# One graph layer on one core: three comparison tiles with a buffer each, the third listed a turn earlier

## The chip, the core and the metric

The kernel runs on one core of one Trainium2 chip. Its time is the device time of one execution in microseconds (us), given as the median of several runs. Below, TensorE is PE, VectorE is DVE, ScalarE is ACT, GpSimd is POOL and the DMA-issuing sync engine is SP, as in the profile.

## What is computed

The reference is one layer of a graph network with a residual and a normalisation. There are 12500 nodes with 128 features, and 400000 edges sorted by their target:

```python
Xs = X[src]
m_data = Xs @ W_data.T + b_data
m_ctrl = Xs @ W_control.T + b_control
msg = jnp.where((edge_types == 0)[:, None], m_data, m_ctrl)
agg = jax.ops.segment_sum(msg, dst, num_segments=X.shape[0])
out = relu(agg + (X @ W_self.T + b_self))
x = layernorm(X + out)
```

Both products are linear, so the kernel sums the raw rows of X first, separately for the two edge types, and multiplies the sums by the weights once for each node.

## The kernel before, in words

**Two ways to fetch a row.** The edges are cut into chunks of 128. Of each 25 chunks, 5 (or, at some places, more) are fetched from memory row by row by indirect DMAs that POOL issues (`msg`, line 825). The other 20 form a *set*, and their rows are picked out of a copy of X that stays in SBUF, by matmuls with 0/1 matrices. There are 107 sets, and the loop `for w in range(pairs)` treats one after the other. Rows are held as three bfloat16 parts, so 128 features are 384 columns.

**Ordering a set.** A set's 2560 edges are first put in order by the 128-row block of X that their source lies in. DVE compares block numbers (`O`, line 533 by way of `block_matrix`), adds up (`prod`, lines 614, 615 and 604), PE counts what stands ahead (line 624), DVE reduces that (`ahead`, line 632) and works out a rank (lines 636 to 645), builds `rm` (line 533) and `rv` (line 676), and PE scatters with them (line 688). ACT copies the result out (`cell`, line 696), SP sends it through memory and spreads it over all partitions (`pick`, line 701), and DVE turns it in place into a 0/1 matrix (`pick`, line 743). This preparation is done two to three sets ahead of use; the last step, line 743, is done during the set before. Edges for which there was no room are found by `key` (line 649) and `top` (line 653), and are moved over by a small chain DVE `over_n` (660), PE (552), DVE `om_all` (558), PE (564), ACT, and one indirect DMA (`both`, line 901) for two sets.

**Using a set.** `picked(w, ...)` makes five turns (`unit(t)`, t from 0 to 4) and an end. `bounds = [0, 5, 10, 15, 19, 24]` are the groups of columns, out of 25, that each turn handles. In turn t:

- PE picks the rows of group t (line 926, four matmuls of 32 output rows for each column) into PSUM tiles `got`, and ACT copies those to SBUF as `emsg` (line 940).
- DVE makes the selection matrices for a number of columns with one comparison each (`choose`, line 917, which calls `select`, line 533): out of `code_col` and the set's `code` it writes a tile `esel` of 128 x (columns x 176). The *first* comparison, listed in turn 0, covers columns 0 to 9 (128x1760). The *second*, in turn 1, covers 10 to 18 (128x1584). The *third*, in turn 3, covers 19 to 24 (128x1056).
- PE adds the previous group's rows into the set's PSUM tile `sums` (line 757, three matmuls a column), with `emsg` and `esel`. Turn 1 reads columns 0 to 4, turn 2 columns 5 to 9, turn 3 columns 10 to 14, turn 4 columns 15 to 18. Columns 19 to 24 are read by the end of the set, `end()`, which the next set's turn 0 calls (`ending()`) after its own first comparison. There DVE also adds `sums` into `acc` (line 814).

**The buffers of the comparisons.** `esel` tiles come from a pool with two buffers for each name. The third comparison takes the buffer of the first of its set, the next set's first that of the second, the next set's second that of the third. A comparison can start when PE has done the last matmul that reads the buffer's previous tile.

**Other work on DVE between them.** The selection matrices of the fetched chunks (`psel`, line 533, 128x1200), their sums and counts (`cnt` and `acc`, line 814), preparation of a group's indices (lines 494 to 515), and finished nodes (lines 1054 to 1071).

**What sets the order.** A program lists the instructions: for each set, several streams (turns, preparation, `pick` of the next set, indices) carry a place between 0 and 1, and `merged` lists them by it. The turns stand at 0.1, 0.3, 0.5, 0.7 and 0.9, the rank chain at 0.31 to 0.35, `O` and lines 614, 615 and 604 at 0.55, line 743 at 0.6, lines 649 and 653 at 0.75. Then a planner of the framework fixes each engine's order when the kernel is compiled: it takes instructions in the listed order, but where the next one is not ready in its plan (an input is missing, a buffer is not free) it takes the first later one that is. `tc.issue_after(...)` forbids some of that: lines 614, 615, 604 and 743 may not come ahead of the latest `rv`. On the chip each engine then keeps the fixed order. The gathers of POOL are gated one by one by matmuls of PE (`paced`).

Of the kernel before, what the change touches and what calls it, by code (L numbers as in the profile page):

```python
# [9 lines left out]
BF = mybir.dt.bfloat16  # L10
# [9 lines left out]
P = 128  # L20
# [17 lines left out]
EW = 88  # L38
# [113 lines left out]
def evenly(units, a=0.0, b=1.0):  # L152
    return [(a + (b - a) * (k + 0.5) / len(units), u) for k, u in enumerate(units)]
# [53 lines left out]
def short_path(ctx, tc, const, ident, eps, wT, brow, bad, x, src, dst, etype, ws, bs, out):  # L207
# [127 lines left out]
    def table(n, base, name):  # L335

        t = keep.tile([P, n], BF, name=name)
        nc.vector.tensor_copy(t, iota([n], [[1, n]], base, 0, f"{name}_i"))
        return t
# [8 lines left out]
    code_col = table(2 * EW, 1, "code_col")  # L348
# [177 lines left out]
    slots, placed = {}, []  # L526
    pairs = len(each_e)

    def select(sel, col, code2):

        rows, n, width = sel.shape
        shape = [rows, n, width // 2, 2]
        nc.vector.tensor_tensor(  # L533
            sel.rearrange("p n (w t) -> p n w t", t=2),
            col[:rows].rearrange("p (o w t) -> p o w t", o=1, t=2).to_broadcast(shape),
            code2.rearrange("p n (o t) -> p n o t", o=1).to_broadcast(shape),
            op=OP.is_equal,
        )
        return sel
# [209 lines left out]
    def sums():  # L749
        return ps2.tile([P, 512], FP, name="sums")  # L750

    def cells_of(ps, width, k):
        return ps[:, k * 2 * width:(k + 1) * 2 * width]

    def add_rows(out, msg, sel, start, stop):
        for j in range(3):
            last = nc.tensor.matmul(  # L757
                out, msg[:, j * D:(j + 1) * D], sel, start=(start and j == 0), stop=stop, skip_group_check=True
            )
        return last  # L760
# [39 lines left out]
    def acc_rows(g, a, b):  # L800
        begin_acc(g)
        return acc[g][:, a:b, :]

    def place_of(g, i):

        parts_in[g] = parts_in.get(g, 0) + 1
        with tc.issue_after(added[-2].ins) if len(added) > 1 else ExitStack():
            return nc.vector.value_load(raw["place"][0:1, g, i:i + 1], min_val=0, max_val=R - WMAX)

    def accumulate(at, rows, ps, wide, width):  # L810

        n = rows.shape[1]
        win = rows[:, :, bass.ds(at, width)]
        added.append(nc.vector.tensor_add(win, win, ps[:, :n * wide].rearrange("p (a w) -> p a w", w=wide)[:, :, :width]))  # L814
# [15 lines left out]
    def paced(now, gate):  # L830

        if spare:
            gather = spare.pop()()
        elif to_fetch and due[len(due) - len(to_fetch)] <= now:
            gather = fetch()
        else:
            return
        tc.add_manual_dep(
            gather.ins, gate.ins.name,
            mybir.DependencyInfo(mybir.DependencyClass.Sync, mybir.DependencyReason.DATA), reason="paced",  # L840
        )
# [8 lines left out]
    def count(ps, sel):  # L850

        for r in range(FAR):
            n = len(range(r, CHUNKS, FAR))
            at = 2 * AW + DPC * r
            for t in range(2):
                nc.tensor.matmul(
                    ps[CAP * t:CAP * (t + 1), at:at + n * PW], one_col[:, :CAP], sel[:, r::FAR, t * PW:(t + 1) * PW],
                    start=False, stop=(r == FAR - 1), skip_group_check=True,
                )
# [35 lines left out]
    def spare_rows(w):  # L895
        n = P if w + 1 < pairs else OVF
        both = two.tile([P, 3 * D], BF, name="both", bufs=1)
        slots[w + 1 if n == P else w]["last"] = both
        if n == P:
            slots[w]["both"] = both  # L900
        return nc.gpsimd.indirect_dma_start(  # L901
            out=both[:n, :], out_offset=None, in_=rows3[:, :],
            in_offset=bass.IndirectOffsetOnAxis(ap=slots[w]["idx"][:n], axis=0),
        )

    def picked(w, tiled, ending, before):

        g, i = each_e[w]  # L910
        s = {"sel": {}, "msg": {}}
        bounds = [0, 5, 10, 15, 19, NQ - 1]
        turns = len(bounds) - 1

        def choose(q0, n):

            sel = select(sp.tile([P, 10, 2 * EW], BF, name="esel")[:, :n], code_col, slots[w]["code"][:, q0:q0 + n])
            for k in range(n):
                s["sel"][q0 + k] = sel[:, k]

        lead = 0 if w % 2 else 2
        half_rows = slice(CAP * lead, CAP * lead + OVF)

        def pick(ps, q, a0=0, a1=4):
            for a in range(a0, a1):
                last = nc.tensor.matmul(  # L926
                    ps[CAP * a:CAP * (a + 1), :], slots[w]["pick"][:, a * NQ + q, :],
                    x3[:, 4 * q + a - a0].rearrange("p j d -> p (j d)"), start=True, stop=True, skip_group_check=True,
                )
            return last  # L930

        def rows(q, n, room, half=False):
            ps = psg.tile([P, room, 512], FP, name=f"got{room}")
            msg = two.tile([P, room, 3 * D], BF, name=f"emsg{room}")
            for k in range(n):
                last = pick(ps[:, k, :3 * D], q + k)
                s["msg"][q + k] = msg[:, k, :]
            if half:
                last = pick(ps[:, n, :3 * D], NQ - 1, lead, lead + 2)
            s["out"] = nc.scalar.copy(msg[:, :n], ps[:, :n, :3 * D])  # L940
            if half:
                nc.scalar.copy(s["msg"][NQ - 1][half_rows, :], ps[half_rows, n, :3 * D])
            return last

        def add(q0, q1):
            done = [
                add_rows(cells_of(s["ps"], EW, 0), s["msg"].pop(q), s["sel"][q], q == 0, q == NQ - 1)
                for q in range(q0, q1)
            ]
            return done[len(done) // 2 - 1], done[-1]  # L950

        def unit(t):

            if t == 3:
                assert not spare
                if "both" in slots[w]:
                    slots[w]["last"] = two.tile([P, 3 * D], BF, name="last", bufs=1)
                s["msg"][NQ - 1] = slots[w]["last"]
            paced(w + (t + 0.5) / turns, rows(bounds[t], 2, 2))
            if t == 1 and w > 0 and w % 2 == 0:  # L960
                spare.append(lambda: spare_rows(w))
            gate = rows(bounds[t] + 2, bounds[t + 1] - bounds[t] - 2, 3, t == 3)
            if t == 0:
                choose(0, 10)
                gates = ending() or [gate]
            if t == 1:
                choose(10, 9)
            if t == 3:
                choose(19, NQ - 19)
            while counts:  # L970
                c = counts.pop(0)
                count(c["ps"], c["sel"])
            if t == 1:
                s["ps"] = sums()
            if t == 1 and before:
                before()
            if t > 0:
                gates = add(bounds[t - 1], bounds[t])
            paced(w + (t + 1) / turns, gates[0])
            if t == 2:  # L980
                paced(w + (t + 1) / turns, gates[-1])
            for u in tiled.get(t, []):
                u()
            if t == 0 and w + 1 < pairs and "own_turn" in slots[w + 1] and w > 0:
                slots[w + 1]["own_turn"]()
            if t == turns - 1 and "both" in slots[w]:
                with tc.issue_after(s["out"].ins):
                    nc.scalar.copy(slots[w]["last"][:OVF, :], slots[w]["both"][:OVF, :])

        def end():  # L990

            early, *more = tiled.get(turns, [lambda: None])
            early()
            gates = add(bounds[turns - 1], NQ)
            for u in more:
                u()
            accumulate(place_of(g, 2 * i + 1), acc_rows(g, 0, 2), s["ps"], EW, EW)
            return gates

        return evenly([lambda t=t: unit(t) for t in range(turns)]), end  # L1000


# [139 lines left out]
    sp = ctx.enter_context(tc.tile_pool(name="sel", bufs=2))  # L1142
# [13 lines left out]
    n = 0  # L1156
# [11 lines left out]
    def ending():  # L1168
        pass
# [191 lines left out]
```

## Time and profile before

| what | value |
|---|---|
| median of 3 runs | 1719.61 us (1719.46 to 1721.19) |
| the profiled execution | 1721.01 us |
| its span, first to last instruction | 1719.3 us |
| granted TensorE clock, mean | 0.994 |
| busy: PE, PE weight loads, DVE, ACT, POOL | 1568.1, 1241.5, 1529.0, 1243.3, 1286.8 us |

The time outside the span is 1721.01 - 1719.3 = 1.7 us. A line such as `L533 DVE TENSOR_TENSOR esel<-code_col,code 128x1760 bf16<-... x321 | 292.9, 913 | 11.8 <-PE sums L757 8.8` reads: line 533, engine DVE, the tile that is written and those that are read, the shape, how many; busy us in all and mean ns of one; then how long the engine sat idle just before these instructions and what ended most of that.

### The profile page before, as it was taken

To read this page: it belongs to the slowest core of one execution; us is meant where nothing else is said; L and a number is where in the kernel's file an instruction comes from. 1 tells how busy PE (TensorE), PEld (TensorE's weight loads), DVE (VectorE), ACT (ScalarE), POOL (GpSimd) and SP (SyncE) were. 2 spreads that over 40 slices of the span, in tenths; PEclk is the share of its full clock that TensorE was granted. 3 is DMA by queue.
4 is the path that set the end of the run, shared out by engine and by line. 5 is a ranking of instruction groups with operands and counts; after the bars stand their busy time and mean duration, and the time that the engine had idled before them with its cause. 6 is when DMAs were issued, how large, how long until landed. Compare 5 with 4: busy or idle time off the path is not lost.

```text
span 1719.3 us, 68641 instructions
## 1 busy us (share of the span) xinstructions
PE 1568.1 (91%) x28525; PEld 1241.5 (72%) x28525; DVE 1529.0 (89%) x3630; ACT 1243.3 (72%) x2198; POOL 1286.8 (75%) x1061
## 2 busy tenths in 40 slices
PE   0599999999999999999899999999999999999997
PEld 0377777777777777777677777777777777777776
DVE  6899899998998989999799899999999899999983
ACT  5777677776777667777576777676777676777675
POOL 0288878888788888888788777777788787777872
PEclk9999999999999999999999999999999999999999
DMA  7844454545444454444445554545544445544442
GB/s 195 280 149 133 126 160 124 147 147 152 134 139 142 139 148 135 140 150 129 144 122 150 160 155 136 152 130 152 150 144 138 135 128 159 155 140 129 138 128 59
DMA packets 148973, 248.30 MB, mean 144 GB/s; under 512 B 35937, under 2 KB 115260, under 8 KB 148652
## 3 DMA queue, kind: packets, MB, share of 16 engines
q1 hardware_dynamic: 85994, 134.45, 23.6%
q0 software_dynamic: 50032, 102.98, 22.2%
q10 hardware_dynamic: 12626, 6.40, 1.4%
q8 instruction: 225, 3.69, 0.9%
q14 instruction: 96, 0.79, 0.1%
HBM read 226.24 MB, written 17.50 MB: 142 GB/s over the span
## 4 chain that ended last, share of the span: by engine, by line
DVE 40%; PE 38%; issue 8%; ACT 5%; DMA 4%; DVEq 1%; POOL 0%; SPq 0%; ACTq 0%; POOLq 0%
PE sums L757 16%; PE got L926 12%; DVE esel L533 5%; DVE prod L641 5%; DVE prod L636 4%; DVE rv L676 3%; DVE pick L743 3%; DVE found L643 3%; PE side L1045 3%; ACT emsg L940 2%; DVE prod L614 2%; PE side L624 2%; DMA both<-rows,idx 2%; DVE psel L533 2%; PE side L688 2%
## 5 line engine op out<-in xcount | busy, mean ns | idle before, releaser
L825 POOL DMA_INDIRECT msg<-rows,idx_g x985 | 1215.5, 1234 | 309.7 <-issue 143.8
L940 ACT CAST emsg<-got 128x768 bf16<-128x768 f32 (+1 forms) x1070 | 949.0, 931 | 296.9 <-PE got L926 277.8
L757 PE MATMUL sums<-esel,emsg 128*128 128x176 bf16 x7704 | 686.6, 240 | 3.4 <-DVE acc L814 2.9
L757 PEld LDWEIGHTS <-emsg 128*128 128x128 bf16 x7704 | 569.5, 98 | 106.1 <-issue 98.8
L926 PE MATMUL got<-x,pick 128*32 128x384 bf16 x10486 | 569.1, 330 | 17.9 <-ACT emsg L940 8.8
L926 PEld LDWEIGHTS <-pick 128*32 128x32 bf16 x10486 | 240.4, 96 | 143.8 <-issue 19.9
L533 DVE TENSOR_TENSOR esel<-code_col,code 128x1760 bf16<-128x1760 bf16 x321 | 292.9, 913 | 11.8 <-PE sums L757 8.8
L757 PE MATMUL sums<-psel,msg 128*128 128x48 bf16 x2955 | 167.2, 184 | 11.8 <-DVE acc L814 9.0
L757 PEld LDWEIGHTS <-msg 128*128 128x128 bf16 x2955 | 138.6, 97 | 21.2 <-issue 16.4
L641 DVE TENSOR_TENSOR prod<-prod 128x1200 bf16<-128x1200 bf16 x214 | 134.0, 626 | 7.2 <-issue 1.1
L533 DVE TENSOR_TENSOR O<-cell_col,blk 128x2000 bf16<-128x2000 bf16 x107 | 128.0, 1197 | 7.1 <-ACT blk L439 4.3
L636 DVE TENSOR_TENSOR prod<-O,ahead 128x2000 bf16<-128x2000 bf16 x107 | 128.3, 1200 | 4.5 <-DVE ahead L632 1.9
L743 DVE TENSOR_SCALAR pick<-pick,lane_f 128x3200 bf16<-128x3200 bf16 x107 | 112.9, 1055 | 0.1
L901 POOL DMA_INDIRECT both<-rows,idx x54 | 66.2, 1226 | 54.4 <-ACT emsg L940 41.8
L688 PE MATMUL side<-rv,O 128*128 128x64 bf16 x2140 | 83.4, 195 | 25.0 <-DVE rv L676 22.1
L533 DVE TENSOR_TENSOR psel<-near_col,near 128x1200 bf16<-128x1200 bf16 x125 | 96.7, 773 | 9.7 <-issue 8.7
L814 DVE TENSOR_TENSOR acc<-acc,sums 128x176 f32 (+2 forms) x232 | 66.8, 288 | 42.1 <-PE sums L757 41.3
L688 PEld LDWEIGHTS <-O 128*128 128x128 bf16 x2140 | 79.0, 100 | 27.2 <-DVE rv L676 22.3
L676 DVE TENSOR_TENSOR rv<-rm,vals 128x1280 bf16<-128x1280 bf16 x107 | 87.9, 822 | 3.3 <-DVE key L649 1.4
L643 DVE TENSOR_REDUCE found<-prod 128x20 f32<-128x600 bf16 x107 | 82.9, 775 | 3.2 <-DVE prod L641 0.4
L614 DVE TENSOR_TENSOR prod<-O 128x1000 bf16<-128x1000 bf16 x107 | 72.0, 673 | 0.0
L624 PEld LDWEIGHTS <-ltri 128*128 128x128 bf16 x1284 | 40.4, 96 | 40.0 <-issue 38.5
(196 smaller groups left out, 1544.6 us busy)
## 6 DMA issues: line engine op xcount, KB each, us to landing
pick<-there SPq DMA_DIRECT2D x106, 800.0 KB
msg<-rows,idx_g POOLq DMA_INDIRECT x985
acc<-acc_start SPq DMA_DIRECT2D x23, 640.0 KB
rows<-x SPq DMA_DIRECT2D x6, 1344.0 KB
xs<-in_x_dram SPq DMA_DIRECT2D x99, 62.5 KB
out_dram<-h SPq DMA_DIRECT2D x99, 62.5 KB
xt<-in_x_dram ACTq DMA_DIRECT2D x6, 896.0 KB
cnt<-cnt_start SPq DMA_DIRECT2D x22, 160.0 KB
```

What stands on the lines that cost most here:

```text
L533: nc.vector.tensor_tensor(sel.rearrange("p n (w t) -> p n w t", t=2), col[:rows].rearrange("p (o w t) -> p o w t", o=1, t=2).to_broadcast( ...
L614: nc.vector.tensor_add(h[:, :2 * CQ], s["O"][:, :2 * CQ], s["O"][:, 2 * CQ:])
L636: nc.vector.tensor_tensor(prod[:, :, :NCELL], s["O"], ahead.rearrange("p (o j) -> p o j", o=1).to_broadcast([P, EC, NCELL]), op=OP.mult,)
L641: nc.vector.tensor_add(prod[:, :, :h], prod[:, :, :h], prod[:, :, h:2 * h])
L643: nc.vector.tensor_reduce(found, prod[:, :, :h], AX.X, OP.add)
L676: placed[:] = [nc.vector.tensor_tensor(rv.rearrange("p c v (r t) -> p c v r t", t=2), rm.rearrange("p c (o r t) -> p c o r t", o=1, t=2).t ...
L688: nc.tensor.matmul(s["rk"][:m, :2 * CAP], s["held"][:, c * NCELL:c * NCELL + m], s["rv"][:, c].rearrange("p v r -> p (v r)"), start=(c == ...
L743: nc.vector.tensor_scalar(t, t, lane_f, None, op0=OP.is_equal)
L757: last = nc.tensor.matmul(out, msg[:, j * D:(j + 1) * D], sel, start=(start and j == 0), stop=stop, skip_group_check=True)
L825: return nc.gpsimd.indirect_dma_start(out=msg, out_offset=None, in_=rows3[:, :], in_offset=bass.IndirectOffsetOnAxis(ap=codes["p", g][0][: ...
L926: last = nc.tensor.matmul(ps[CAP * a:CAP * (a + 1), :], slots[w]["pick"][:, a * NQ + q, :], x3[:, 4 * q + a - a0].rearrange("p j d -> p (j ...
L940: s["out"] = nc.scalar.copy(msg[:, :n], ps[:, :n, :3 * D])
```

## The change

The `esel` tiles get three buffers in place of two, so each of a set's three comparisons always has the same buffer, and shares it only with the same comparison of other sets. The third comparison is listed in turn 2 in place of turn 3. Nothing else is edited.

```diff
         def choose(q0, n):
-            sel = select(sp.tile([P, 10, 2 * EW], BF, name="esel")[:, :n], code_col, slots[w]["code"][:, q0:q0 + n])
+            sel = select(sp.tile([P, 10, 2 * EW], BF, name="esel", bufs=3)[:, :n], code_col, slots[w]["code"][:, q0:q0 + n])
...
             if t == 1:
                 choose(10, 9)
-            if t == 3:
+            if t == 2:
                 choose(19, NQ - 19)
```

## The prediction

> **What bounds the kernel now.** I read the page's busy times first, then the busy time of each engine in the steady stretch from 100 to 1700 us, then what PE and DVE waited for there, and last one set in the timeline. Below, A, B and C are the first, second and third comparison of a set.
>
> ```profile
> PE 1568.1 (91%) x28525; PEld 1241.5 (72%) x28525; DVE 1529.0 (89%) x3630; ACT 1243.3 (72%) x2198; POOL 1286.8 (75%) x1061
> ```
> ```profile
> 100.00:1700.00 1600.00, 1516.43 (x27774) 1203.50 (x27772) 1443.90 (x3373) 1168.69 (x2092) 1262.46 (x1024) 0.99 0.47 141
> ```
>
> In the steady stretch PE is idle for 1600 - 1516 = 84 us, 5%; DVE for 156 us. Time can only be won where PE idles, and it is lost wherever DVE makes PE wait longer. So the next view is what PE waited for in that stretch (us in all, times, longest):
>
> ```profile
> PE side L709 <- ACT cell L696: 19.2, 12, 6.3
> PE sums L757 <- DVE acc L814: 12.0, 19, 1.1
> PE side L504 <- DVE code_r L496: 11.6, 17, 1.1
> PE got L926 <- DVE pick L743: 8.1, 17, 1.0
> PE got L926 <- ACT emsg L940: 7.5, 22, 0.6
> PE side L564 <- DVE om_all L558: 6.4, 21, 0.7
> PE side L552 <- DVE over_n L660: 3.9, 6, 0.9
> ```
>
> No row has `esel`: PE never waits for a comparison. It waits, by half a us at a time, for what DVE does after them: `pick`, `om_all`, `over_n`, `code_r`, `acc`. DVE's own waits in the stretch:
>
> ```profile
> DVE acc L814 <- PE sums L757: 40.4, 35, 7.7
> DVE ahead L632 <- PE side L624: 30.3, 53, 1.6
> DVE esel L533 <- PE sums L757: 8.8, 20, 2.1
> ```
>
> The wait that the change removes is the last, 8.8 us in 20 times. Here is what DVE did in a set without other work, from its start to the start of the next (start, duration, and in brackets the idle time before it and what ended that, where it was 0.15 us or more):
>
> ```profile
> 1235.64 1.06 DVE L533 TENSOR_TENSOR esel<-code_col,code 128x1760 bf16<-128x1760 bf16 x1
> 1236.63 1.22 DVE L533 TENSOR_TENSOR O<-cell_col,blk 128x2000 bf16<-128x2000 bf16 x1
> 1237.77 0.39 DVE L558 TENSOR_SCALAR om_all<-slot_col,side 128x70 bf16<-128x70 bf16 x2
> 1238.08 0.33 DVE L814 TENSOR_TENSOR acc<-acc,sums 128x176 f32 x1
> 1238.33 0.97 DVE L533 TENSOR_TENSOR esel<-code_col,code 128x1584 bf16<-128x1584 bf16 x1
> 1240.26 0.37 DVE L632 TENSOR_REDUCE ahead<-side 128x100 bf16<-128x200 f32 x1 [0.96 <-PE side L624]
> ...
> 1244.26 0.49 DVE L533 TENSOR_TENSOR rm<-rank_col,rank 128x640 bf16<-128x640 bf16 x1
> 1244.66 0.70 DVE L533 TENSOR_TENSOR esel<-code_col,code 128x1056 bf16<-128x1056 bf16 x1
> 1245.28 0.82 DVE L676 TENSOR_TENSOR rv<-rm,vals 128x1280 bf16<-128x1280 bf16 x1
> ...
> 1247.22 1.05 DVE L743 TENSOR_SCALAR pick<-pick,lane_f 128x3200 bf16<-128x3200 bf16 x1
> 1248.19 0.17 DVE L649 SCALAR_TENSOR_TENSOR key<-rank,pk 128x20 f32<-128x20 bf16 x1
> ...
> 1248.49 1.06 DVE L533 TENSOR_TENSOR esel<-code_col,code 128x1760 bf16<-128x1760 bf16 x1
> ```
>
> and from PE's rows of that stretch (the last matmul group of turn 2, that of turn 4, the first use of the next set's `pick`):
>
> ```profile
> 1238.22 0.51 PE L564 MATMUL side<-bits_b,om_all 128*128 128x3 bf16 x14 [0.37 <-DVE om_all L558]
> ...
> 1242.38 1.31 PE L757 MATMUL sums<-esel,emsg 128*128 128x176 bf16 x15
> ...
> 1247.03 1.08 PE L757 MATMUL sums<-esel,emsg 128*128 128x176 bf16 x12
> ...
> 1248.80 1.00 PE L926 MATMUL got<-x,pick 128*32 128x384 bf16 x20
> ```
>
> Two things are to be seen. The listed order isn't DVE's: `O`, listed at 0.55, runs right behind A, and C, listed behind `pick`, stands ahead of `rv`. The planner pulls forward whatever is ready when the next in the list isn't. And DVE is a close second bound: `pick` ends at 1247.22 + 1.05 = 1248.27, PE needs it at 1248.80, a cover of 0.53 us; 17 sets have none (the row of L926 and L743 above).
>
> **The change part by part.** Durations are the means of these groups:
>
> ```profile
> L533 DVE TENSOR_TENSOR O<-cell_col,blk 128x2000 bf16<-128x2000 bf16 x107 | 128.0, 1197 | 7.1 <-ACT blk L439 4.3 <-issue 1.5 <-PE side L552 0.8
> L533 DVE TENSOR_TENSOR esel<-code_col,code 128x1760 bf16<-128x1760 bf16 x107 | 113.7, 1062 | 5.4 <-PE sums L757 2.8 <-PE side L688 1.0 <-PE side L709 0.5
> L533 DVE TENSOR_TENSOR esel<-code_col,code 128x1584 bf16<-128x1584 bf16 x107 | 104.4, 975 | 0.1
> L533 DVE TENSOR_TENSOR esel<-code_col,code 128x1056 bf16<-128x1056 bf16 x107 | 75.0, 701 | 6.2 <-PE sums L757 6.0
> ```
>
> No instruction is added or removed and none changes its shape; no DMA is issued by the moved step, and it passes only DVE's queue. What changes is when each comparison may start. C waited for turn 2's matmuls, which read A (1242.38 + 1.31 = 1243.69), and started at 1244.66, at the first opening behind that. Now it waits for the previous set's end, as `acc` does: it may run from 1238.4 on. The *next* set's A waited for turn 4's matmuls, which read B (1247.03 + 1.08 = 1248.11); now it waits for turn 2's, so it may run from 1243.69 on, inside this set's rank chain. B waited for the end's matmuls; now for turn 4's, so it may run ahead of `acc`.
>
> 1. *The waits of `esel`*, 8.8 us, go. C's part, 6.0 us, lies ahead of `rv` and `pick`. PE gains only where `pick` has no cover, 17 of 106 sets, and little cover in some more: I count a quarter, -1.5 us (bounds 0 and -8.8).
>
> The Trainium skill, Perfetto Trace Analysis, § Optimization Strategy, says that the same gap repeating on the engine that should be saturated can mean that there isn't enough SBUF for the next tile, that is, too few buffers. By that rule the extra buffer would be worth those 8.8 us, 1719.6 - 8.8 = 1710.8. The rows of PE's waits speak against it, as the gap is DVE's.
>
> 2. *C leaves the chain, B and O change places.* C's 0.70 us disappear ahead of `rv`. B, listed ahead of `O`, now takes the place ahead of `acc`. Behind `acc` then stand C and O, 0.70 + 1.20 = 1.90 us, where B's 0.975 stood: +0.92. Where DVE idles ahead of `ahead` that is hidden: 30.3 us in 53 waits, 0.57 in each, 0.29 as a mean over 106 sets. So `pick` moves by -0.70 + 0.92 - 0.29 = -0.07 us, say -0.06. (Where O stays ahead of `acc` it is -0.70; where no idle hides O, +0.22.)
>
> 3. *A is pulled into the chain of the set before.* No row shows that, since its buffer wasn't free. Nearest is C, which waited for just the same matmuls: in this stretch it stands inside the chain. Where A takes that place, `pick` is 1.06 us later. From below: never, as line 649 (0.17 us) is listed ahead of A and can fill the opening between `rm` and `rv`. From above: in every set. I take 0.4 of the sets: nearest to the row of C, less what line 649 takes. `pick` moves by +0.42 us in the mean.
>
> 4. *What that costs.* Together `pick` is 0.36 us later. In 17 sets without cover that is 17 x 0.36 = 6.1 us. For the other 89 I estimate a cover spread evenly from 0 to 1 us around the 0.53 read above: 89 x 0.36 x 0.36 / 2 = 5.8 us. `code_r` stands behind `rv` and moves too, in sets that partly pay already: 17 x 0.36 / 2 = 3.1 us.
>
> 5. *What it gives back.* An A that ran early no longer stands ahead of `om_all` and `over_n`: 0.4 of (6.4 + 3.9) = -4.1 us. In the others B for O makes `om_all` 0.22 us earlier: 0.6 x 21 x 0.22 = -2.8 us. What of `acc` gets late behind B is inside the 40.4 us that DVE waits there: 0, with a cost of B's 0.975 in sets where DVE arrives late.
>
> Sum: -1.5 + 6.1 + 5.8 + 3.1 - 4.1 - 2.8 = **+6.6 us**. The profiled execution is 1721.0 us (span 1719.3 + 1.7 outside), 1.4 above the median, so it would become 1727.6, and the median 1719.6 + 6.6 = **1726 us**, 0.4% slower. If A is pulled forward in 0.6 of the sets (`pick` +0.58), the same sum is 9.9 + 15.0 + 4.9 - 6.2 - 1.9 - 1.5 = +20, 1740 us. In none it is -1.0 - 4.6 - 1.5 = -7, 1712.5 us. It changes sign at about a quarter of the sets.
>
> **The rivals.**
>
> - *Faster: C fills real idle time.* C goes into the idle before `ahead`, O stays ahead of `acc`, and A stays behind `pick`. Then `pick` and `code_r` are 0.70 us earlier in the half of the sets that have that idle; half of PE's 8.1 and 11.6 us goes, with the 4.6 and 1.5 from above: -4 - 5 - 4.6 - 1.5 = -15, so 1705 to 1712, middle **1708**. For it: 30.3 us of idle at just that place. Against: gains end where PE's waits end, and the planner fills openings that the chip doesn't have as readily as real ones (C at 1244.66 stands in one behind `rm`, which ends at 1244.26 + 0.49 = 1244.75). It decides when A overtakes `pick` in under a quarter of the sets.
> - *No change.* C has long been ahead of `pick`, so its new place in the list does nothing, and A, B and O only trade places within cover: within 3.4 us of **1719.6**.
> - *Much slower: B and O both ahead of `om_all`.* PE stands 0.37 us at L564 for it in the quoted set. With another 0.975 us ahead, in half of the 53 sets that have it (one chain for two sets): +26, **1745**. For it: `om_all` is just in time. Against: one comparison already fills the opening that O filled.
> - *DVE is the bound.* Then all idle that C can fill counts: 8.8 + 30.3 = 39, **1680**. Against: PE is idle for 5% only.
>
> The Trainium skill, Perfetto Trace Analysis, § Identifying the Most-Contended Engine, would have PE judged by its weight loads' busy share and DVE by its occupancy: 72% against 89%, which makes DVE the bound, as in the last rival. The idle time of PE's row, 84 of 1600 us, doesn't agree.
>
> **How the numbers follow.** Forecast (slower, 1720 to 1742 around 1726): 0.40. Faster by filled idle: 0.30. No change: 0.18. Much slower: 0.08. DVE-bound: 0.04. A measurement here tells about 0.2% (3.4 us) from no change. Faster by more than that: 0.30 + 0.04 = 0.34; within: 0.18; slower: 0.40 + 0.08 = 0.48. The range, 1705 to 1742, holds the forecast with its bound of 0.6, no change, and most of the faster case; it leaves out the DVE-bound case, the lower tail of the faster one (0.07), the upper half of the much slower one and the forecast's tail (0.09): 2 in 10. Slower cases alone: 1723 to 1742.
>
> **What would show it.** Right: the idle of `esel` behind L757 near 0; C directly behind `acc` or in the first openings of the chain; A of the next set ahead of `pick` in some 40 sets; PE's waits for `pick` and `code_r` up from 19.7 to some 30 us, those for `om_all` and `over_n` down. Wrong: A never overtakes `pick` and idle ahead of `ahead` falls well below 30 us (faster), or L564's wait grows by 20 us (much slower). A different order of the gathers on POOL, which gate `cell` (19.2 us in 12 waits, one of 6.3), could move the time by as much as all of this and is not in the sum.

## The result, and the profile after

The changed kernel takes 1743.78 us (median of 5 runs, 1741.62 to 1744.06), the kernel before 1719.61 (1719.26 to 1724.21). The ratio is **1.0133** (95% interval 1.0119 to 1.0147): 1.3% slower, +24 us where +6.6 was forecast, and outside the range. The profiled execution is 1742.83 us with a span of 1741.1.

The page's busy times after:

```profile
PE 1570.9 (90%) x28525; PEld 1240.0 (71%) x28525; DVE 1529.0 (88%) x3630; ACT 1244.3 (71%) x2198; POOL 1316.6 (76%) x1061
```

PE, DVE and ACT do what they did before, to within 3 us. POOL, with the same 1061 instructions, is busy 1316.6 us where it was 1286.8: +29.8 us. No step of the forecast had that. The steady stretch, from 100 us to about 20 us ahead of the end as before:

```profile
100.00:1720.00 1620.00, 1518.69 (x27814) 1202.03 (x27807) 1444.81 (x3376) 1170.56 (x2096) 1292.08 (x1025) 0.99 0.47 139
```

PE is idle for 1620 - 1518.7 = 101 us there, 18 more than before. What PE waited for in that stretch (us in all, times, longest):

```profile
PE side L709 <- ACT cell L696: 31.8, 28, 3.8
PE got L926 <- DVE pick L743: 15.7, 20, 1.4
PE side L504 <- DVE code_r L496: 12.7, 17, 0.9
PE sums L757 <- DVE acc L814: 11.8, 20, 1.1
...
PE side L564 <- DVE om_all L558: 6.8, 23, 1.2
PE side L552 <- DVE over_n L660: 3.1, 7, 0.5
```

The waits for `pick` and `code_r` rose from 19.7 to 28.4 us; the forecast's signs said some 30. The largest rise is another: `cell`, from 19.2 to 31.8. DVE's own waits in the stretch:

```profile
DVE acc L814 <- PE sums L757: 34.4, 37, 5.3
DVE ahead L632 <- PE side L624: 27.2, 48, 1.6
DVE esel L533 <- ACT code L576: 17.3, 24, 1.3
...
DVE esel L533 <- PE sums L757: 6.3, 15, 1.4
```

The comparisons' wait for PE's matmuls, which free the buffers, fell from 8.8 to 6.3 us only, and a new one of 17.3 us for their input (`code`) stands beside it: they now come so early that the input isn't there.

Here is DVE in a plain set after the change (start, duration, idle before it and what ended that):

```profile
1241.55 1.06 DVE L533 TENSOR_TENSOR esel<-code_col,code 128x1760 bf16<-128x1760 bf16 x1
1242.53 0.18 DVE L645 CAST rank<-found 128x40 bf16<-128x40 f32 x1
1242.74 0.49 DVE L533 TENSOR_TENSOR rm<-rank_col,rank 128x640 bf16<-128x640 bf16 x1
...
1243.26 0.82 DVE L676 TENSOR_TENSOR rv<-rm,vals 128x1280 bf16<-128x1280 bf16 x1
...
1245.21 1.04 DVE L743 TENSOR_SCALAR pick<-pick,lane_f 128x3200 bf16<-128x3200 bf16 x1
...
1246.96 0.97 DVE L533 TENSOR_TENSOR esel<-code_col,code 128x1584 bf16<-128x1584 bf16 x1
1247.85 1.19 DVE L533 TENSOR_TENSOR O<-cell_col,blk 128x2000 bf16<-128x2000 bf16 x1
...
1249.27 0.33 DVE L814 TENSOR_TENSOR acc<-acc,sums 128x176 f32 x1
1250.30 0.71 DVE L533 TENSOR_TENSOR esel<-code_col,code 128x1056 bf16<-128x1056 bf16 x1 [0.70 <-ACT code L576]
1251.45 0.36 DVE L632 TENSOR_REDUCE ahead<-side 128x100 bf16<-128x200 f32 x1 [0.44 <-PE side L624]
```

All three comparisons moved as steps 2 and 3 said: A (128x1760) into the rank chain, ahead of `rv` and so of `pick`; B (128x1584) ahead of the previous set's `acc`; C (128x1056) right behind `acc`. Counted over the traces, A is ahead of `pick` and of `rv` in 90 of 107 sets (before: none), B ahead of `acc` in 106 (none), C ahead of `ahead` in 104 (none).

**What the forecast had not looked at** is POOL's row of gathers. Its columns are busy us, mean ns of one, and the idle time just ahead of them; before, then after:

```profile
L825 POOL DMA_INDIRECT msg<-rows,idx_g x985 | 1215.5, 1234 | 309.7 <-issue 143.8
```
```profile
L825 POOL DMA_INDIRECT msg<-rows,idx_g x985 | 1244.1, 1263 | 302.4 <-issue 137.8
```

Before, each of the 985 gathers has 309.7 / 985 = 0.314 us of idle ahead of it, after 0.307. That is nearly a constant, and the timeline of POOL after the change shows it (idle ahead in brackets):

```profile
1245.21 1.16 POOL L825 DMA_INDIRECT msg<-rows,idx_g  x1 [0.30 <-PE sums L757]
1246.68 0.95 POOL L825 DMA_INDIRECT msg<-rows,idx_g  x1 [0.30 <-issue]
1247.93 1.93 POOL L825 DMA_INDIRECT msg<-rows,idx_g  x1 [0.30 <-PE side L552]
1250.16 0.94 POOL L825 DMA_INDIRECT msg<-rows,idx_g  x1 [0.30 <-PE side L564]
1251.41 0.94 POOL L825 DMA_INDIRECT msg<-rows,idx_g  x1 [0.30 <-PE side L624]
```

Whatever releaser the row names, the gap is 0.30 us. So one gather follows the other as closely as POOL can, and the named gate was open long before. From 100 us to 35 us ahead of the end the gathers (`msg`, and `both` of line 901) last 1289 us (before 1259), the 1022 gaps of 0.305 us between them take 312 us, and only 5 us of idle are left beyond those (before 14). POOL, 76% busy by the page, has no room. (The page's own list of the chain that ended last gives POOL 0% before and 1% after; it doesn't show this. The runs below that load and unload POOL do.) Over the whole span the gathers' time rose by 1244.1 - 1215.5 = 28.6 us, their idle fell by 7.3, together **+21.3 us; the span rose by 1741.1 - 1719.3 = 21.8**.

PE feels this through `both`. ACT's copy of `both` (`last`, line 988) waits for the transfer, and `cell` stands behind it on ACT, PE's line 709 behind `cell`. One of them, rows of ACT and then of PE:

```profile
1166.59 0.51 ACT L988 COPY last<-both 64x384 bf16<-64x384 bf16 x1 [3.36 <-DMA both<-rows,idx]
1167.01 0.20 ACT L696 CAST cell<-side 128x64 bf16<-128x64 f32 x1
```
```profile
1167.26 0.20 PE L709 MATMUL side<-ident_b,cell 128*32 128x25 bf16 x4 [2.58 <-ACT cell L696]
```

In 12 of the 28 waits for `cell` ACT had just stood so, and they make 24.5 of the 31.8 us (before 18.4 of 19.2): the larger part of what PE's waits call `cell` is a gather that lands late. Of the rise of 12.6 us it is about half; the other half is many short waits behind other work of ACT.

**Why the gathers last longer.** The shape is the same in both kernels; the shortest take 0.94 us. They take that where DVE is idle. Near the end of the kernel before, DVE does nothing from 1683.70 (the end of a C) to 1687.59, and POOL's rows there are

```profile
1683.85 0.94 POOL L825 DMA_INDIRECT msg<-rows,idx_g  x1 [0.30 <-issue]
1685.10 0.94 POOL L825 DMA_INDIRECT msg<-rows,idx_g  x1 [0.30 <-PE got L926]
1686.34 0.94 POOL L825 DMA_INDIRECT msg<-rows,idx_g  x1 [0.30 <-issue]
```

while the gather of 1.93 us above starts at 1247.93, 0.08 us into the `O` that starts at 1247.85. Grouping the gathers of the kernel before (from 100 us on) by what DVE runs when each starts gives the mean time beyond 0.943 us:

| DVE runs at the gather's start | gathers | beyond 0.943 us, mean |
|---|---|---|
| nothing | 89 | 0.00 |
| `found` (line 643) | 17 | 0.00 |
| `acc` | 37 | 0.09 |
| `ahead` (line 632) | 36 | 0.15 |
| `prod` (lines 615 and 641) | 122 | 0.16 |
| C | 52 | 0.21 |
| `rm` | 57 | 0.27 |
| B | 65 | 0.29 |
| `pick` (line 743) | 47 | 0.30 |
| `rv` (line 676) | 73 | 0.31 |
| `prod` (line 636) | 94 | 0.44 |
| `psel` | 39 | 0.48 |
| `O` | 54 | 0.49 |
| A | 89 | 0.58 |
| line 614 | 31 | 0.65 |
| `worst` (line 499) | 16 | 1.53 |

(The other groups have at most 16 gathers each.) The sum beyond 0.943 us is 297 us before and 325 after. So the order of DVE's operations, which have not changed, sets how long POOL takes over the same gathers. This table is of one trace, and no run took such an operation away; what the runs varied is the order.

The traces say more, gather by gather. A gather that starts while `esel`, `O`, `psel`, `rm`, `rv`, `prod` or `pick` runs on DVE lasts 0.943 us plus what is left of that operation, less 0.12 us; any other lasts 0.943 us. In the gather above, `O` ends at 1247.85 + 1.19 = 1249.04, 1.11 us after the gather's start: 0.943 + 1.11 - 0.12 = 1.93 us, as measured. This gives 878 of the 1023 gathers of the kernel before to within 0.04 us and 867 of 1024 after, where a constant 0.943 us gives 325 and 368. Nearly all others last longer than by this rule (138 before, 148 after), the 16 beside `worst` among them. By this a gather waits for the end of the operation that it finds running on DVE; it is read from the traces, and no run varied it alone.

The Trainium skill, SBUF — State Buffer, § SBUF: two separate sides, says that DVE and GpSimd share a pair of ports under an exclusive lock, which some DVE operations hold for the whole instruction (among them those with two SBUF inputs, against a GpSimd operation that reads SBUF), and that a DMA issued from POOL needs its descriptors written by GpSimd. The table agrees as far as it goes: 0.00 beside an idle DVE and beside `found`, which has one input, 0.09 beside `acc`, most of which have one input in PSUM, 0.16 to 0.65 beside the comparisons, `rv` and `prod` with their two inputs. `pick`, with one wide input and a value per partition, has 0.30; by which kind of lock, no run shows.

### The profile page after: what moved, and what is told of

Same layout as the page of the kernel before. It is cut to its first block, busy times and chain, and to the rows that moved or that the text cites. A ratio compares the mean times of both kernels' runs of the same rounds, so it can differ in the third digit from the quotient of the medians.

```text
span 1741.1 us, 68575 instructions
## 1 busy us (share of the span) xinstructions
PE 1570.9 (90%) x28525; PEld 1240.0 (71%) x28525; DVE 1529.0 (88%) x3630; ACT 1244.3 (71%) x2198; POOL 1316.6 (76%) x1061
## 4 chain that ended last, share of the span: by engine, by line
DVE 43%; PE 35%; issue 7%; ACT 6%; DMA 4%; DVEq 2%; POOL 1%; SPq 0%; ACTq 0%; POOLq 0%
PE sums L757 15%; PE got L926 11%; DVE esel L533 6%; DVE prod L641 5%; DVE prod L636 4%; DVE pick L743 4%; DVE rv L676 3%; PE side L1045 3%; DVE found L643 3%; DMA both<-rows,idx 3%; DVE prod L614 2%; ACT emsg L940 2%; DVE psel L533 2%; PE side L624 2%; DVE O L533 2%
## 5 line engine op out<-in xcount | busy, mean ns | idle before, releaser
L825 POOL DMA_INDIRECT msg<-rows,idx_g x985 | 1244.1, 1263 | 302.4 <-issue 137.8
L926 PE MATMUL got<-x,pick 128*32 128x384 bf16 x10486 | 569.1, 330 | 26.8 <-DVE pick L743 15.7
L533 DVE TENSOR_TENSOR esel<-code_col,code 128x1760 bf16<-128x1760 bf16 x321 | 293.2, 914 | 42.9 <-ACT code L576 17.3
L757 PE MATMUL sums<-psel,msg 128*128 128x48 bf16 x2955 | 165.3, 184 | 14.1 <-DVE acc L814 10.4
L757 PEld LDWEIGHTS <-msg 128*128 128x128 bf16 x2955 | 137.9, 97 | 22.0 <-issue 18.4
L688 PEld LDWEIGHTS <-O 128*128 128x128 bf16 x2140 | 78.8, 100 | 26.1 <-DVE rv L676 22.4
```

The lines of the kernel that those rows point to most:

```text
L533: nc.vector.tensor_tensor(sel.rearrange("p n (w t) -> p n w t", t=2), col[:rows].rearrange("p (o w t) -> p o w t", o=1, t=2).to_broadcast( ...
L688: nc.tensor.matmul(s["rk"][:m, :2 * CAP], s["held"][:, c * NCELL:c * NCELL + m], s["rv"][:, c].rearrange("p v r -> p (v r)"), start=(c == ...
L757: last = nc.tensor.matmul(out, msg[:, j * D:(j + 1) * D], sel, start=(start and j == 0), stop=stop, skip_group_check=True)
L825: return nc.gpsimd.indirect_dma_start(out=msg, out_offset=None, in_=rows3[:, :], in_offset=bass.IndirectOffsetOnAxis(ap=codes["p", g][0][: ...
L926: last = nc.tensor.matmul(ps[CAP * a:CAP * (a + 1), :], slots[w]["pick"][:, a * NQ + q, :], x3[:, 4 * q + a - a0].rearrange("p j d -> p (j ...
```

## The experiments

**The theories.** The *first*, the forecast's: the freed buffers let A and B run early, A stands inside the chain, `pick` is late, PE waits. The *second*, its rival: the earlier place of C costs it. The *third* was first only a chance shift of POOL's gathers, seen in PE's wait for `cell`; from the runs with fewer and more gathers on it is this: POOL has no room, and the new order of DVE makes the gathers longer. In rows of the experiments the line numbers are up to 8 higher than before, by the lines added. The first four ran on a chip where the kernel before takes 1996 us (PE's clock 0.97; in these four POOL is idle 0.57 to 0.59 us ahead of a gather in place of 0.31), and are shown beside their repeats on chips where it takes 1716 to 1722 us, as in all later runs.

**The two halves of the change.** Three buffers alone:

```diff
-            sel = select(sp.tile([P, 10, 2 * EW], BF, name="esel")[:, :n], ...
+            sel = select(sp.tile([P, 10, 2 * EW], BF, name="esel", bufs=3)[:, :n], ...
```

> The third buffer alone; the third comparison stays listed in turn 3. Theory 1 (the third buffer lets the next set's first comparison run inside the rank chain, ahead of rv and pick, so pick comes up to 1.06 us later and PE waits): the first comparison again stands ahead of rv in most sets, and the time is that of the changed kernel, 1738 to 1748 us. Theory 2 (it is the third comparison's earlier place behind acc that costs): near the kernel before, 1716 to 1724. Theory 3 (it is a chance shift of POOL's gathers, seen as PE's wait for cell at L709): the time follows L709's wait alone, 20 us or 32 us.

> The third buffer alone again, since the four runs before were on a chip where the kernel before takes 1996 us and PE itself is the bound. Theory 1 (the third buffer lets the next set's first comparison run ahead of rv and pick; pick is late and PE waits): 1735 to 1748 us where the kernel before takes 1720. Theory 2 (the third comparison's earlier place costs): 1716 to 1724. Theory 3 (a chance shift of the gathers, seen as PE's wait for cell at L709): as L709's wait falls out, 20 or 32 us.

C listed in turn 2 alone, with two buffers:

```diff
-            if t == 3:
+            if t == 2:
                 choose(19, NQ - 19)
```

> The third comparison listed in turn 2, still two buffers. Theory 1: the first comparison still waits for turn 4's matmuls and can't overtake pick, the third still for turn 2's; so 1716 to 1724 us. Theory 2: 1735 to 1748 us. Theory 3: as L709's wait falls out.

> The listing in turn 2 alone, two buffers, on a chip where DVE is a close second bound. Theory 1: the third comparison still waits for turn 2's matmuls and the first for turn 4's, so 1716 to 1724 us. Theory 2: 1730 to 1745 us. Theory 3: as L709's wait falls out.

Buffers alone: ratio 1.0123 (1.0102 to 1.0144), 1745.08 against 1720.88 us; on the other chip 1.0023 (1.0005 to 1.0042). The turn alone: 0.9987 (0.9973 to 1.0000), there 1.0011 (0.9988 to 1.0033). So the buffers are the whole cost and the listing does next to nothing. With buffers alone DVE's order is that of the whole change in what matters: A is again ahead of `pick` in 90 sets, and PE waits 16.3 us for it. That the same edit costs 1.2% on one chip and 0.2% on the other doesn't tell the theories apart: there POOL has room (63% busy), but DVE has too (77%), and PE waits only 3.9 us for `pick` with the buffers alone.

**Holding comparisons behind other work.** The framework's `issue_after` adds a pure order on DVE. After the change, A held behind `pick` (line 743):

```diff
+                turned[:] = [nc.vector.tensor_scalar(t, t, lane_f, None, op0=OP.is_equal)]
...
-                choose(0, 10)
+                with tc.issue_after(turned[0].ins):
+                    choose(0, 10)
```

> The changed kernel, but the first comparison may not be placed ahead of its set's pick step (line 743). Theory 1: pick ends about 1 us earlier in the plain sets, PE's wait for pick falls from 15.7 us to 8 or less, and the time is 1710 to 1722 us. Theory 2: no gain, 1738 to 1748 us. Theory 3: L709's wait stays about 32 us and the time at 1732 or more.

> The changed kernel with the first comparison kept behind its set's pick step (line 743), again, on a chip where DVE is a close second bound. Theory 1: 1708 to 1722 us beside 1720 of the kernel before, PE's wait for pick 8 us or less. Theory 2: 1738 to 1748 us. Theory 3: L709's wait stays about 32 us and the time at 1732 or more.

A and C held behind `pick`, C listed in turn 3 again:

```diff
-            if t == 2:
-                choose(19, NQ - 19)
+            if t == 3:
+                with tc.issue_after(turned[0].ins):
+                    choose(19, NQ - 19)
```

> Three buffers, third comparison listed in turn 3, first and third both kept behind the pick step of line 743. Theory 1: pick 0.7 us earlier than before in most sets, PE's waits for pick near 0: 1703 to 1716 us. Theory 2: 1716 to 1724 us. Theory 3: follows L709's wait, 20 us (1720) or 32 us (1732).

A held behind `pick` and B behind the previous set's `acc`, C free; and B alone held:

```diff
-                choose(10, 9)
+                with tc.issue_after(ended[0].ins) if ended else ExitStack():
+                    choose(10, 9)
...
+            ended[:] = added[-1:]
```

> The changed kernel with the first comparison kept behind its set's pick step and the second behind the acc of the set before, so that of the three new freedoms only the third comparison's is left: it runs behind the second, ahead of ahead. Theory 1 (two pulled-forward comparisons cost: the first makes pick late, the second makes over_n and om_all late): all of the loss goes, and the third comparison fills idle: 1708 to 1722 us beside 1720 of the kernel before. Theory 2 (the third comparison's earlier place costs what is left, 7 us): 1725 to 1732. Theory 3: as L709's wait for cell falls out, 20 us or 32 us.

> The changed kernel with the second comparison alone kept behind the acc of the set before; the first is free to run ahead of rv and pick. Theory 1: the first comparison's part alone: PE's wait for pick stays at 14 us or more, those for om_all and over_n at 10 us or less; 1732 to 1742 us. Theory 2: 1725 to 1732. Theory 3: as L709's wait falls out.

The kernel before with two buffers, and only C held behind `pick`:

```diff
             if t == 3:
-                choose(19, NQ - 19)
+                with tc.issue_after(turned[0].ins):
+                    choose(19, NQ - 19)
```

> The kernel before, but the third comparison may not be placed ahead of the next set's pick step (line 743). Theory 1 in its general form (whatever stands ahead of pick costs PE where pick has no cover): pick 0.7 us earlier in most sets, PE's 8.1 us of waits for pick and part of code_r's 11.6 go: 1704 to 1715 us. Theory 2 says nothing of it: 1716 to 1724 us.

> The kernel before (two buffers) with the third comparison kept behind the next set's pick step, on a chip where DVE is a close second bound. Theory 1: pick up to 0.7 us earlier, PE's waits for pick (8.1) and some for code_r (11.6) go, while over_n behind it may come 0.7 us later: 1708 to 1720 us. Theory 2: 1716 to 1724 us.

| kernel | us | ratio to before (95%) | PE's wait for `pick`, us |
|---|---|---|---|
| before | 1719.61 | 1 | 8.1 |
| after | 1743.78 | 1.0133 (1.0119 to 1.0147) | 15.7 |
| A held | 1728.68 | 1.0042 (1.0029 to 1.0054) | 2.6 |
| A and C held | 1734.09 | 1.0065 (1.0048 to 1.0082) | 3.1 |
| A and B held | 1750.21 | 1.0165 (1.0145 to 1.0186) | 4.1 |
| B held | 1752.18 | 1.0165 (1.0144 to 1.0185) | 26.2 |
| before, C held | 1711.20 | 0.9938 (0.9923 to 0.9953) | 4.0 |

Each ratio is to the kernel before on the same chip, 1719.6 to 1721.9 us. On the other chip, A held came to 0.9992 (0.9961 to 1.0024) and the kernel before with C held to 0.9950 (0.9929 to 0.9971).

Holding A takes away two thirds of the loss, as the first theory wants, though not down to the 1708 to 1722 us that it gave. The kernels with A and C, A and B, and B alone held came out slower than any of the theories had said ahead of the runs (at most 1732, 1732 and 1742 us). The one with A and B held breaks the first theory. There `pick` is earlier than in the kernel before (4.1 us of waits where that has 8.1), and the kernel is the slower one by 1.65%. PE's waits there:

```profile
PE side L709 <- ACT cell L696: 53.1, 31, 5.9
...
PE got L929 <- DVE pick L745: 4.1, 9, 0.8
```

The time has gone to `cell`, behind `both`. (With A and C held it stands elsewhere: PE waits 21.2 us for `over_n`, 3.9 before, and 18.8 for `cell`, since A and C now run ahead of `over_n`. The gathers are 18.3 us longer there as well, and that run alone doesn't tell the two causes apart.) The row of gathers, of this kernel, then of the kernel before with C held:

```profile
L828 POOL DMA_INDIRECT msg<-rows,idx_g x985 | 1248.2, 1267 | 307.8 <-issue 138.3 <-PE got L929 66.5 <-PE sums L760 54.6
```
```profile
L827 POOL DMA_INDIRECT msg<-rows,idx_g x985 | 1210.3, 1229 | 303.6 <-issue 128.0 <-PE sums L759 69.0 <-PE got L928 52.9
```

The gathers of the slow kernel last 1.267 us in the mean, those of the fast one 1.229. Taking busy time and idle of this one row, against 1215.5 + 309.7 = 1525.2 before, and the spans against 1719.3:

| kernel | gathers, us | idle ahead, us | change of the sum | change of the span |
|---|---|---|---|---|
| after | 1244.1 | 302.4 | +21.3 | +21.8 |
| three buffers alone | 1238.8 | 313.6 | +27.2 | +26.3 |
| turn alone | 1221.6 | 307.4 | +3.8 | +0.6 |
| A held | 1231.4 | 300.7 | +6.9 | +3.4 |
| A and C held | 1233.8 | 310.9 | +19.5 | +15.7 |
| A and B held | 1248.2 | 307.8 | +30.8 | +27.9 |
| B held | 1246.2 | 311.9 | +32.9 | +33.6 |
| before, C held | 1210.3 | 303.6 | -11.3 | -11.4 |

Busy and idle of an engine always add up to about the span, so the last two columns alone show little. What tells is the third column: the idle stays within 5% of 985 x 0.305 = 300 us whatever PE and DVE do, and the busy time carries the rest. PE's wait for `pick` is no guide to which kernel is slower. (PE's granted clock was 0.986 and 0.987 in the two slowest, 0.991 to 0.995 in the others; with A and B held PE is busy 1570.2 us, after 1570.9, so the clock doesn't make that kernel slow; with B held it is 1579.7, and some of that loss may be PE's.)

**Loading and unloading POOL.** If POOL is the bound, more gathers cost time though no other engine has more to do, and fewer bring time back until the next engine binds. To the kernel before, one gather more at every twentieth chunk, of the same rows into a tile that nobody reads:

```diff
+        if len(to_fetch) % 20 == 0:
+            twin = mp.tile([P, 3 * D], BF, name="twin", bufs=2)
+            nc.gpsimd.indirect_dma_start(
+                out=twin, out_offset=None, in_=rows3[:, :], ...
```

> The kernel before with one gather in twenty issued twice, the second copy into a tile that nobody reads: 50 gathers more on POOL, nothing on PE, DVE and ACT. Theory 3: 50 x (1.23 + 0.3) = 77 us more, 1775 to 1800 us. Theory 1 (POOL is 75% busy and has room): 1718 to 1730 us.

Measured: 1776.51 us against 1716.17, ratio 1.0356 (1.0323 to 1.0389): some 60 us for 50 gathers, 51 in the profiled executions. The two rows of POOL:

```profile
L831 POOL DMA_INDIRECT msg<-rows,idx_g x985 | 1193.2, 1211 | 307.8 <-issue 139.6 <-PE got L932 59.2 <-PE sums L757 51.8
L827 POOL DMA_INDIRECT twin<-rows,idx_g x50 | 63.6, 1273 | 15.2 <-issue 9.2 <-DMA msg<-rows,idx_g 1.5 <-ACT vals L439 1.2
```

The twins take 63.6 + 15.2 = 78.8 us, and the other gathers became 22.3 us shorter, their idle 1.9: +54.6 in all. No instruction was added on another engine, and PE paid again at line 709, where it had waited 19.2 us (100 to 1750 us):

```profile
PE side L709 <- ACT cell L696: 59.5, 23, 9.5
```

The other way, a quarter of the gathers left out (those chunks' matmuls read the previous chunk's rows), in the kernel before, in the kernel after, and with A and B held:

```diff
+        if len(to_fetch) % 4 == 0 and len(fetched) > 0:
+            fetched.append(fetched[-1])
+            return None
```

> The kernel before with one gather of msg in four left out; that chunk's matmuls read the previous chunk's rows, so all other engines' work stays and its sums are those of other rows. Theory 1 (DVE's chain to pick, and PE's waits for it, set the time): 1712 to 1722 us. Theory 3 in its new form (POOL is the bound: gathers back to back, 0.305 us between them, so time is the sum of their durations): 246 gathers of 1.23 + 0.3 us less; POOL stops being the bound and the time falls by 15 us or more, to 1640 to 1705 us.

> The changed kernel with one gather of msg in four left out in the same way. Theory 1: the loss stays, 1735 to 1748 us, 20 us or more above the kernel before with the same left out. Theory 3 (POOL-bound; the changed order of DVE makes gathers longer): the loss goes with the bound, within 10 us of the other, 1640 to 1710 us.

> The kernel with first and second comparisons held back and the third free (1750 us with all gathers), with one gather of msg in four left out in the same way. Theory 3: without POOL as bound, its smaller waits of PE for DVE count: at or below the kernel before with the same left out, 1630 to 1700 us. If its loss were DVE's or PE's own: 1735 us or more.

| kernel, a quarter of the gathers left out | us | ratio to before (95%) | PE's wait for `pick` |
|---|---|---|---|
| before | 1693.85 | 0.9866 (0.9839 to 0.9893) | 8.8 |
| after | 1708.79 | 0.9953 (0.9938 to 0.9969) | 15.5 |
| A and B held | 1687.74 | 0.9824 (0.9798 to 0.9851) | 6.2 |

In the first of them the row of gathers is

```profile
L828 POOL DMA_INDIRECT msg<-rows,idx_g x739 | 906.5, 1227 | 519.2 <-PE got L931 243.8 <-PE sums L757 186.7 <-issue 79.2
```

0.70 us of idle ahead of each, ended by PE's matmuls: POOL now waits for its gates. In this regime the first theory holds. The changed order costs 1708.79 - 1693.85 = 15 us; its span is 13.3 us longer, and PE waits 6.7 us longer for `pick`, 4.1 for `cell`, 1.2 for `code_r` and 1.0 for `acc`, with smaller rises and falls beside these. (The third theory had expected 10 us or less.) The gathers last as long as with all of them, 1.227, 1.260 and 1.267 us in the mean for the three orders: their length comes from the order, and not from a full POOL. And holding A and B, which was the slower by 28 us with all gathers, is here the faster by 6. DVE's order is the same in both (A ahead of `pick` in 90 sets after, in none with A and B held). **The same order of DVE has the opposite sign by which engine binds.**

**Order, or the place of the tiles?** A third buffer also moves tiles in SBUF. The kernel before with a pad of that buffer's size (its one small write is made once, at the start), and the kernel after with all three comparisons held near the places they had before (C behind `rm`):

```diff
+    pad = sp.tile([P, 10, 2 * EW], BF, name="pad", bufs=1)
+    nc.vector.memset(pad[:, 0, 0:2], 0.0)
```
```diff
-            if t == 2:
-                choose(19, NQ - 19)
+            if t == 3:
+                with tc.issue_after(ranked[0].ins):
+                    choose(19, NQ - 19)
```

> The kernel before, its order of instructions unchanged, with an idle tile of the size of one comparison buffer in the same pool (one memset of two columns), so that what lies behind it in SBUF moves as it does in the changed kernel. If gathers get longer because of where tiles lie: mean gather 1.25 us or more and 1735 to 1750 us. If they get longer because of the order on DVE: mean gather 1.23 to 1.24 us and 1714 to 1724 us.

> Three buffers, but first, second and third comparison held to about the places they have in the kernel before (behind the pick step, behind acc, behind rm). If the order on DVE is what counts (forecast's cause and longer gathers both follow from it): mean gather 1.23 to 1.24 us, 1714 to 1726 us. If the third buffer itself costs (place in SBUF, or the comparisons no longer waiting for PE): 1735 us or more.

The pad gives 1.0010 (0.9993 to 1.0027), three buffers in about the old order 1.0030 (1.0009 to 1.0051). Gathers of the latter:

```profile
L830 POOL DMA_INDIRECT msg<-rows,idx_g x985 | 1215.2, 1234 | 314.0 <-issue 146.0 <-PE got L931 68.3 <-PE sums L762 53.6
```

They last 1.234 us in the mean, as before. So the place of the tiles costs nothing that can be measured, and the buffers cost by the order that they permit; the 0.3% left in the second is not taken apart further. Between this kernel and that with A and B held only the place and listing of C differ, and the gathers by 1248.2 - 1215.2 = 33 us.

**What stays open** is which property of an order makes the gathers longer. In both kernels of the last comparison DVE does the same operations, and the excess over 0.943 us is 328 us in one and 296 in the other. The rule above (a gather waits for the operation that it finds running) gives 240 and 232 of these, so 8 of the 32 us of difference; between before and after it gives 14 of 28. The rest lies in the gathers that last longer than by the rule. The runs show that the order sets the length, and only in part by what rule.

## Why the prediction was wrong, by its own steps

The direction was right, and most of the mechanism that it named takes place. By PE's rows 8.7 us of the loss stand at `pick` and `code_r`. But with POOL full these rows don't set the time: with A and B held they come to 14.1 us, where the kernel before has 19.7, and that kernel is 28 us slower.

- **What bounds the kernel: this step failed.** "Time can only be won where PE idles, and it is lost wherever DVE makes PE wait longer" left out POOL, 75% busy by the page. Its own window row had 1262.46 us busy in 1024 instructions; with 0.305 us between them that is 1262 + 312 = 1574 of 1600 us. The last sentence of the prediction named the gathers and `cell`, "could move the time by as much as all of this", and left them out of the sum, that is, put them at nothing without a reason. In place of 0 the runs showed +28.6 us of gathers, with 7.3 us less idle ahead of them: 21.3 of the 21.8 us of the span. (What it named was another order of the gathers; they became longer.)
- **Step 1, the waits of `esel`, -1.5 us.** The wait for PE's matmuls went down by 2.5 us, not 8.8, and the comparisons waited 17.3 us for `code`. No row of PE has `esel`, before or after; whether the step was worth its 1.5 us, no run shows.
- **Step 2, C leaves the chain, B and O change places.** C did leave the place between `rm` and `rv`, and B did come ahead of `acc`. But O did not go behind `acc`: it stands between `acc` and `pick` in 11 of 104 steady sets (before in 17 of 103). In that interval B's 0.98 us went and A's 0.91 (a mean over all sets) came; C, in it before with 0.61, is in it with 0.70.
- **Step 3, A in the chain in 0.4 of the sets.** It was 0.84 (90 of 107). The row of C, which stood inside the chain in the quoted set, was the better guide, and the discount for line 649 was wrong.
- **Step 4, the price.** From the end of `acc` to that of `pick` it takes 0.23 us longer (10.63 for 10.40, means of the steady sets), not 0.36 or, with a share of 0.84, 0.83. With 0.23 the step's formula gives 17 x 0.23 + 89 x 0.23 x 0.23 / 2 = 6.3 us for `pick`, and +7.6 was measured; `code_r` 2.0, measured +1.1. The formula held. The forecast's own terms here add up to 15.0 us (its signs, from 19.7 to some 30, fit only 10), and 8.7 were measured. With the true share and the forecast's own step 2 the formula would have given 45 us for `pick` alone: two errors nearly cancelled, and that the size came out near is luck.
- **Step 5, the give-back.** `om_all` went from 6.4 to 6.8 and `over_n` from 3.9 to 3.1 us: -0.4 in place of -6.9.
- **The rivals.** *Much slower* (1745) came out near the time for another reason: line 564's wait, which was to grow by 20 us, grew by 0.4. *DVE is the bound*, *faster* and *no change* are refuted by the time.
- **What it came from.** With room on POOL the change costs 13 to 15 us (the pair with a quarter of the gathers left out): the kind of loss that was forecast, at about twice its size. With POOL full the longer gathers decide. What the change would cost with a full POOL and gathers of the old length, no run shows.

The rule on too few buffers of the Trainium skill (Perfetto Trace Analysis, § Optimization Strategy), weighed in step 1, gave 1710.8; the runs speak against it here: the extra buffers alone cost 1.2%, and the version that beat both kernels, 0.9938 (0.9923 to 0.9953), has two buffers and more order. It holds C behind `pick`, which halves PE's wait for `pick` and takes 5 us off the gathers.

## What to carry to other kernels

Before an engine is given room by its busy share, divide the idle time ahead of its commonest instruction by their count: a constant (0.31 us here) that no releaser changes is part of the instruction's cost, and count x (duration + constant) may fill the span at 75% busy. A buffer more is also a freedom more for whoever plans the order; if it pulls work into the chain that the next stage waits for, an explicit order with fewer buffers can be the faster kernel. Judge a new order by what it does to the engine that binds, and take load off that engine once to see which one it is.

## What the runs showed of the hardware

- Between two indirect gathers of POOL lie at least 0.30 us (median 0.305 or 0.306 in every run, minimum 0.303), whatever the gate.
- The same gather of 128 rows takes 0.94 us where DVE is idle at its start. Where it starts while one of the seven kinds of DVE operation named above runs, it lasts longer by what is left of that operation less 0.12 us (within 0.04 us in 86% of the gathers of the kernel before, by this rule); the longest there took 4.51 us. The order of unchanged DVE operations moves the mean of 985 gathers from 1.229 to 1.267 us: 38 us in 1720.
- On the chip of the first four runs PE is 84 to 85%, DVE 77 to 78% and POOL 63% busy; the gathers took 1.19 us in the mean, and the third buffer alone cost 0.2% in place of 1.2%.
